# A selective scan between two feed-forward layers: one scan instruction over two rows, group sums on GpSimd, and a planner's constants with them

## The chip, the cores and the metric

The kernel runs on one core of one Trainium2 chip, in float32. The metric is the device time of one execution in microseconds (us). The kernel before has a median of 2821.96 us over 3 runs.

## What is computed

Each of the 4 x 1024 tokens has 512 values. The reference adds half of a feed-forward layer to them, then a selective state-space layer, then half of the same feed-forward layer again:

```python
x = x + 0.5 * ffn(layernorm(x))
x = x + attn(layernorm(x))
x = x + 0.5 * ffn(layernorm(x))
# ffn: silu(x @ gate_w.T * gate_s) * (x @ up_w.T * up_s) @ down_w.T * down_s,  512 -> 1408 -> 512
# attn: h, gate = split(W_in x);  h = silu(causal conv of 4 taps over time);  (ts, B, C) = rms(Wx h)
#       delta = softplus(Wdt ts + bias);  for each channel i (1024) and state n (16), over time t:
#       s[i,n] = exp(delta[i,t] * A[i,n]) * s[i,n] + delta[i,t] * B[n,t] * h[i,t]
#       y[i,t] = sum_n s[i,n] * C[n,t] + D[i] * h[i,t];   out = Wout (y * silu(gate))
```

## The kernel before

The tokens are cut into 16 chunks of 256 (T), four to a sequence. A chunk of the state-space layer is prepared (`prep`: layer norm, transposes, input projection `hp`, convolution, `sp` for ts, B and C; `heads`: delta and delta*h, called dd, written to DRAM rows and read back as `rep`, so that each of four groups of 32 partitions holds 32 channels for four of the 16 states), then scanned (`scan`), then projected back (`tail`).

In `scan` a chunk has 8 channel tiles i. A tile has 4 groups g and, in a group, 4 rows h of 256 time steps. For two rows at a time:
- ACT makes the decays (L841), one exponential for each row, into a PSUM bank `da`; there are three such banks.
- POOL (GpSimd) makes delta*h*B, 128x512, into `sb` (L848).
- DVE scans each row in place (L857, `tensor_tensor_scan`), starting from 0 in the first chunk of a sequence and from the kept state else; keeps the last column of both rows as state (L867), unless it is the last chunk of a sequence; and multiplies by C (L874).
- POOL adds the product of an odd group to that of the even group before it (L882).

What is left of a tile are two sums of 4 rows. PE folds them (L891): for either sum and each row one matmul with a 128x32 matrix adds up the four partition groups, so 8 matmuls of 256 columns into the bank `yps`, that is kept for this alone. A float32 matmul leaves two records in the profile. DVE adds D*h (L903), POOL multiplies by the gate (L909).

The feed-forward layers run in 17 passes (ORDER) over two chunks of either layer: gate products (L414), evicted by ACT (L429), Silu over `hd` in three parts (SILUS), up products (L414), evicted by DVE (L452), and the down product by Strassen's scheme (L539, L555), whose sums and differences of `hd` POOL makes (L506). DVE adds the results to x (L578). Their layer norms (`normed`) take for each tile of 128 tokens statistics on DVE (L332, L333), three tiny operations on POOL (L337 to L339), scale and shift on ACT (L350), a transpose on PE (L343) and an eviction on ACT (L358). PE's projections, the passes and the folds share four PSUM banks (class `mm`).

The order on each engine is set by a planner at build time. Every operation has an engine, a cost, what it reads and writes, and a due time; a scan unit is due by PACE, a pass by FFN_END. The planner takes the operation that can start first and, among those, the one due first; HOT is due before all others. Buffers are of classes with so many slots each (SLOTS). The result is one fixed order for each engine, in which an operation that must wait holds up what stands behind it. All transfers but the small constants are issued by SP, in the planner's order.

Of the kernel before, what the change touches and what calls it, by code (L numbers as in the profile page):

```python
# [9 lines left out]
F32 = mybir.dt.float32  # L10
AF = mybir.ActivationFunctionType
ALU = mybir.AluOpType
# [25 lines left out]
for _p in range(7, 14, 2):  # L38
    ORDER += [[(1, _p), (1, _p + 1)], [(2, _p - 6), (2, _p - 5)]]
ORDER += [[(2, _p), (2, _p + 1)] for _p in range(9, 14, 2)] + [[(2, 15)]]  # L40
SILUS = (4, 8, 11)
SLOTS = dict(
    mm=4, da=3, rf=12, rm=6, px=14, xf=4, xi=2, xo=1, xn=3, ss=2, sm=8, sr=4, u=2, dd=2, rep=2, bc=2, sn=2, sq=1, row=8, bcd=2, tsT=1, bcT=1, xnT=1,
)
PACE = 153
# [4 lines left out]
FFN_END = 2650  # L50
FLIPS = 16
HOT = -1e9

# [126 lines left out]
def macaron_kernel(ctx: ExitStack, tc: tile.TileContext, a: dict, out: bass.AP):  # L180
# [7 lines left out]
    yps = banks.tile([P, 2, T], F32, name="yps")  # L188
    ident = const.tile([P, P], F32, name="ident")
    make_identity(nc, ident)  # L190
    neg_half = const.tile([P, 4], F32, name="neg_half")
    nc.gpsimd.memset(neg_half, -0.5)
    fold = const.tile([P, Q], F32, name="fold")
# [86 lines left out]
    def scale_down(down, due):  # L280
        ds2 = Buf("px", "ds2", [P, 2, T])

        def flat():
            return ds2.tile.rearrange("p a t -> p (a t)")
# [35 lines left out]
    def normed(x, at_x, name, due, flipped):  # L320
        sm = Buf("sm", f"sm{name}", [P, 16])
        xn = Buf("xn", f"xn{name}", [P, H])
        tp = mm(f"tp{name}")
        m, q = (sm, 0), (sm, 1)

        def parts():
            s = sm.tile
            return s[:, 0:6], s[:, 6:8], s[:, 8:9], s[:, 9:10], s[:, 10:11]

        def spread():  # L330
            stt, mv, *_ = parts()
            pin(nc.vector.bn_stats(stt, at_x()))  # L332
            pin(nc.vector.bn_aggr(mv, stt))  # L333

        def roots():
            _, mv, ve, rs, nb = parts()
            pin(nc.gpsimd.tensor_scalar(ve, mv[:, 1:2], EPS, None, ALU.add))  # L337
            pin(nc.gpsimd.tensor_tensor(rs, ve, neg_half[:, 0:1], ALU.pow))
            pin(nc.gpsimd.tensor_scalar(nb, mv[:, 0:1], rs, -1.0, ALU.mult, ALU.mult))  # L339

        def turned():
            for k in range(KH):
                pin(nc.tensor.transpose(tp.tile[:, k * P : (k + 1) * P], xn.tile[:, k * P : (k + 1) * P], ident))  # L343

        dst, w, more = flipped
        op("DVE", 0.65, spread, x, [m], due - 9, name=f"stats{name}")
        op("POOL", 1.0, roots, [m], [q], due - 8, name=f"roots{name}")
        op(
            "ACT", 0.71,
            lambda: pin(nc.scalar.activation(  # L350
                xn.tile, at_x(), AF.Identity, bias=sm.tile[:, 10:11], scale=sm.tile[:, 9:10],
            )),
            list(x) + [q], [xn] + w, due - 4, name=f"xn{name}",
        )
        op("PE", 0.45, turned, [xn], [tp], due - 2, name=f"flip{name}")

        def out_of():
            pin(nc.scalar.copy(dst(), tp.tile.rearrange("p (k t) -> p k t", k=KH)))  # L358
            if more:
                more()  # L360

        op("ACT", 0.48, out_of, [tp], w, HOT, name=f"unflip{name}")

# [18 lines left out]
    def ffn(n):  # L382
# [13 lines left out]
        for v, (stage, p) in enumerate(of):  # L396
            x = x_of[p] if stage == 2 and p in x_of else Buf("xf", f"x{name}_{v}", [P, 2, H])
            pairs.append(x)
            for m in range(J):
                t, r = J * v + m, J * p + m  # L400
                due = ffn_due(base[0]) - FLIPS - 3 * (W4 - t)
                if x.cls == "xf":
# [4 lines left out]
                normed(  # L407
                    quads(x, m), lambda x=x, m=m: x.tile[:, m, :], f"{name}_{t}", due,
                    (lambda t=t: fxT[:, :, t * P : (t + 1) * P], [("fxT", t)], None),
                )  # L410
# [11 lines left out]
        for it in range(NF):  # L422
# [9 lines left out]
                [gp], [("hd", it, t) for t in ts], HOT, name=f"ungate{name}_{it}",  # L432
# [55 lines left out]
    def split_down(name, tiles, pairs, spend):  # L488
# [21 lines left out]
        for r0, r1 in ((0, 3), (3, K1)):  # L510
            q0, q1 = r0 + K1, r1 + K1
            n = r1 - r0
            v1, v2 = (lambda r0=r0, r1=r1: s1.tile[:, r0:r1, :hw]), (lambda r0=r0, r1=r1: s2.tile[:, r0:r1, :hw])
            a11, a21 = (lambda r0=r0, r1=r1: h_at(r0, r1, 0)), (lambda r0=r0, r1=r1: h_at(r0, r1, 1))
            a12, a22 = (lambda q0=q0, q1=q1: h_at(q0, q1, 0)), (lambda q0=q0, q1=q1: h_at(q0, q1, 1))
            combine(v1, a21, a22, ALU.add, h_of(r0, r1, 1) + h_of(q0, q1, 1), s_of(s1, r0, r1), n, t0 - 4 + r0, "s1")
            combine(v2, v1, a11, ALU.subtract, h_of(r0, r1, 0) + s_of(s1, r0, r1), s_of(s2, r0, r1), n, t0 + 3 + r0, "s2")
            combine(a21, a11, a21, ALU.subtract, h_of(r0, r1, 0) + h_of(r0, r1, 1), h_of(r0, r1, 1), n, t0 + 8 + r0, "s3")
# [85 lines left out]
        for r0, r1 in ((0, 3), (3, K1)):  # L604
# [3 lines left out]
                ALU.subtract, h_of(q0, q1, 0) + s_of(s2, r0, r1), h_of(q0, q1, 0), r1 - r0, t0 + 15 + r0, "s4",  # L608
# [31 lines left out]
    def prep(k):  # L640
        d = st[k]
        base = at(k - 1, 7) if k else 70.0
        xT = d["xnT"] = Buf("xnT", f"xnT{k}", [P, KH, K - 1 + T])
        for j in range(J):
# [4 lines left out]

            def edges(j=j):  # L650
# [7 lines left out]
            o = K - 1 + j * P  # L658
            normed([x], lambda x=x: x.tile, f"m{k}_{j}", base + 2 * j, (lambda o=o: xT.tile[:, :, o : o + P], [(xT, j)], None))
            op("POOL", 0.3, edges, [(xT, 1)] if j else [], [("back",)] if j else [(xT, 0), ("back",)], HOT, name=f"edges{k}_{j}")  # L660
        u = d["u"] = Buf("u", f"u{k}", [P, NI, T])
        for i in range(NI):
# [9 lines left out]
            op("ACT", 0.45, first, [hp], [(u, i)], HOT, name=f"tap{k}_{i}")  # L672
# [16 lines left out]
        sr = [Buf("sr", f"sr{k}_{j}", [P, 8]) for j in range(J)]  # L689
# [12 lines left out]
        for j in range(J):  # L702
            def squares(j=j):
                v = sp.tile.rearrange("p (j t) -> p j t", j=J)
                for q, (o, m) in enumerate(parts):
                    pin(nc.scalar.activation(sq.tile[:, o : o + m], v[:, j, o : o + m], AF.Square, accum_out=sr[j].tile[:, q : q + 1]))

            def powers(j=j):
                ss, rr = sr[j].tile[:, 0:3], sr[j].tile[:, 4:7]
                pin(nc.gpsimd.tensor_scalar(ss[:, 0:1], ss[:, 0:1], 1.0 / R, EPS, ALU.mult, ALU.add))  # L710
                pin(nc.gpsimd.tensor_scalar(ss[:, 1:3], ss[:, 1:3], 1.0 / N, EPS, ALU.mult, ALU.add))
                pin(nc.gpsimd.tensor_tensor(rr, ss, neg_half[:, 0:3], ALU.pow))

            def weigh(j=j):
                v = sp.tile.rearrange("p (j t) -> p j t", j=J)
                for q, (o, m) in enumerate(parts):
                    pin(nc.vector.scalar_tensor_tensor(
                        sn[j].tile[:, o : o + m], v[:, j, o : o + m], sr[j].tile[:, 4 + q : 5 + q], ln_w[:, o : o + m], ALU.mult, ALU.mult,
                    ))

            op("ACT", 0.6, squares, [sp], [sq, (sr[j], 0)], HOT, name=f"sq{k}_{j}")
            op("POOL", 1.4, powers, [(sr[j], 0)], [(sr[j], 1)], HOT, name=f"rr{k}_{j}")
            op("DVE", 0.54, weigh, [sp, (sr[j], 1)], [sn[j]], HOT, name=f"sn{k}_{j}")
# [82 lines left out]
    def gates(k):  # L806
        for i in range(NI):
# [5 lines left out]
                [gp], [("g", i)], HOT, name=f"ung{k}_{i}",  # L813
# [7 lines left out]
    def scan(k):  # L821
# [4 lines left out]
        for i in range(NI):  # L826
# [3 lines left out]
            made_of = []  # L830
            for g in range(NS):
                due = at(k, i * NS + g)
                for h in range(0, S, 2):
# [3 lines left out]
                    sb = Buf("px", f"sb{nm}", [P, 2, T])  # L837
                    for j in range(2):
# [7 lines left out]
                    behind("dbu", op(  # L846
                        "POOL", 1.23,
                        lambda sb=sb, h=h, g=g, rep=rep: pin(nc.gpsimd.tensor_tensor(  # L848
                            sb.tile, rep.tile[:, h : h + 2, 1, :], bc.tile[:, g : g + 1, :].to_broadcast([P, 2, T]), ALU.mult,
                        )),  # L850
                        reps + bcs, [(sb, 0), (sb, 1)], due - 6, after=last_of("dbu"), name=f"dbu{nm}",
                    ))
# [202 lines left out]
```

## Time and profile before

| what | value |
|---|---|
| median of 3 runs | 2821.96 us (2820.63 to 2824.64) |
| the profiled execution | 2822.59 us |
| its span, first to last instruction | 2820.8 us |
| PE busy | 2768.3 us |
| DVE busy | 2543.7 us |
| POOL busy | 2395.0 us |
| ACT busy | 1756.3 us |
| mean granted TensorE clock | 0.994 |

The span is what the profile covers, and all shares are of it. PE is TensorE's matmuls, PEld its weight loads, DVE VectorE, ACT ScalarE, POOL GpSimd, SP the engine that issues transfers. A row such as "L857 DVE TENSOR_TENSOR_SCAN da<-da,state,sb ... x1536 | 1090.8, 741" is a group of instructions of line 857: what it writes and reads, its count, the time in which at least one of them was busy, and the mean record of one in ns. Records of one engine overlap by some 0.08 us on DVE, so a group's busy time over its count is less than the mean; what one instruction occupies is best read from start to start in the timeline. A wait line gives the waiting engine and line, whom it waited for, the total in us, how often, and the longest.

### The profile page before, as it was taken

Reading aid. Unit: us, or ns where it says so; the run is one execution under the profiler, and the core shown is the slowest. Engines: PE = TensorE matmul, PEld = TensorE weight load, DVE = VectorE, ACT = ScalarE, POOL = GpSimd, SP = SyncE. Lnnn points to the kernel's source line nnn. Section 1 sums busy time; section 2 is a strip of 40 time slices with the busy share of each in tenths; the row PEclk is TensorE's granted clock in tenths of the full one; section 3 lists DMA queues with packets and bytes.
Section 4 is the critical chain, followed back from the end, with each engine's and each line's share of the span. In section 5 each row is a group of like instructions: output and inputs, shape, how many; then the busy total and the mean of one; then the engine's idle time right before and its main releaser. Section 6 shows DMA issues by size and latency. Waiting matters only on the chain.

```text
span 2820.8 us, 38816 instructions
## 1 busy us (share of the span) xinstructions
PE 2768.3 (98%) x11278; PEld 1733.2 (61%) x11278; DVE 2543.7 (90%) x5088; ACT 1756.3 (62%) x3286; POOL 2395.0 (85%) x2279
## 2 busy tenths in 40 slices
PE   8998999999999999999999999999999999999999
PEld 6565575575655755647557565575665756657458
DVE  3289899999999999999999999999999999999861
ACT  2356667667567585676666766668567576674821
POOL 1189899899898989899899999899899998989951
PEclk9999999999999999999999999999999999999999
DMA  8576667676576666866757667666676775766635
GB/s 263 168 206 178 168 184 219 185 214 197 148 236 158 202 185 172 233 160 189 206 162 236 168 185 207 196 175 194 173 224 173 219 208 153 211 165 176 175 102 155
DMA packets 304691, 531.01 MB, mean 188 GB/s; under 512 B 34016, under 2 KB 58720, under 8 KB 304480
## 3 DMA queue, kind: packets, MB, share of 16 engines
q1 hardware_dynamic: 303040, 528.35, 66.5%
q8 instruction: 90, 1.47, 0.2%
q14 instruction: 121, 0.99, 0.1%
q10 hardware_dynamic: 1440, 0.19, 0.0%
HBM read 464.84 MB, written 63.57 MB: 187 GB/s over the span
## 4 chain that ended last, share of the span: by engine, by line
PE 43%; DVE 35%; issue 7%; ACT 7%; POOL 5%; DMA 3%; SPq 0%; ACTq 0%; DVEq 0%; POOLq 0%
DVE da L857 21%; PE upf L414 11%; PE gatef L414 11%; DVE sb L874 6%; PE hp L633 3%; PE gp L633 3%; PE op L930 2%; PE paf L539 2%; POOL sb L848 2%; ACT da L841 2%; DVE u L676 2%; PE yps L891 2%; PE pcf L539 2%; DMA rep<-row 2%; PE pbf L539 1%
## 5 line engine op out<-in xcount | busy, mean ns | idle before, releaser
L841 ACT ACTIVATE da<-rep,a_w 128x256 f32<-128x256 f32 x2048 | 964.7, 476 | 794.8 <-DVE sb L874 734.4
L848 POOL TENSOR_TENSOR sb<-rep,bc 128x512 f32<-128x512 f32 x1024 | 1284.1, 1280 | 81.5 <-DMA rep<-row 59.2
L857 DVE TENSOR_TENSOR_SCAN da<-da,state,sb 128x256 f32<-128x256 f32 x1536 | 1090.8, 741 | 49.6 <-ACT da L841 29.5
L882 POOL TENSOR_TENSOR sb<-sb,sb 128x512 f32<-128x512 f32 x512 | 651.5, 1278 | 84.9 <-DVE sb L874 83.1
L874 DVE TENSOR_TENSOR sb<-da,bc 128x512 f32<-128x512 f32 x1024 | 692.8, 677 | 0.5
L414 PE MATMUL gatef<-fxT,w_gate_w 128*128 128x512 f32 (+1 forms) x1496 | 632.7, 574 | 5.1 <-ACT dd L772 3.0
L414 PE MATMUL upf<-fxT,w_up_w 128*128 128x512 f32 (+1 forms) x1496 | 624.3, 569 | 0.5 <-DVE u L676 0.5
L414 PEld LDWEIGHTS gatef<-fxT,w_gate_w 128*128 128x128 f32 x1496 | 284.5, 192 | 294.7 <-issue 267.6
L414 PEld LDWEIGHTS upf<-fxT,w_up_w 128*128 128x128 f32 x1496 | 280.9, 190 | 290.9 <-issue 268.0
L857 DVE TENSOR_TENSOR_SCAN da<-da,sb 128x256 f32<-128x256 f32 x512 | 333.5, 681 | 22.6 <-ACT da L841 19.5
L633 PE MATMUL hp<-xnT,w_W_in 128*128 128x259 f32 x1024 | 238.6, 383 | 4.3 <-ACT fxT L358 1.5
L633 PE MATMUL gp<-xnT,w_W_in 128*128 128x256 f32 x1024 | 241.1, 380 | 0.2 <-ACT fxT L358 0.2
L633 PEld LDWEIGHTS hp<-xnT,w_W_in 128*128 128x128 f32 x1024 | 192.4, 190 | 61.3 <-issue 20.1
L633 PEld LDWEIGHTS gp<-xnT,w_W_in 128*128 128x128 f32 x1024 | 191.9, 189 | 61.0 <-issue 28.4
L930 PE MATMUL op<-w_Wout,u 128*128 128x512 f32 x512 | 229.3, 594 | 0.0
L452 DVE SCALAR_TENSOR_TENSOR hd<-upf,up_s,hd 128x512 f32<-128x512 f32 (+1 forms) x187 | 131.0, 701 | 59.4 <-PE upf L414 59.4
L676 DVE SCALAR_TENSOR_TENSOR u<-hp,conv_w,u 128x256 f32<-128x256 f32 x384 | 171.9, 468 | 6.0 <-ACT u L668 5.3
L429 ACT ACTIVATE hd<-gatef,gate_s 128x512 f32<-128x512 f32 (+1 forms) x187 | 121.8, 652 | 64.0 <-PE gatef L414 63.8
L930 PEld LDWEIGHTS op<-w_Wout,u 128*128 128x128 f32 x512 | 95.8, 190 | 105.2 <-issue 99.4
L891 PE MATMUL yps<-sb,fold 128*32 128x256 f32 x2048 | 141.1, 387 | 0.6 <-POOL sb L882 0.5
L539 PE MATMUL paf<-w_half,hd 128*128 128x256 f32 x620 | 141.0, 380 | 0.0
L539 PEld LDWEIGHTS paf<-w_half,hd 128*128 128x128 f32 x620 | 117.1, 190 | 22.0 <-issue 4.4
(104 smaller groups left out, 2911.1 us busy)
## 6 DMA issues: line engine op xcount, KB each, us to landing
rep<-row SPq DMA_DIRECT2D x512, 256.0 KB, 5.0
w_half<-sd SPq DMA_DIRECT2D x272, 256.0 KB, 3.0
w_W_in<-in_W_in_dram SPq DMA_DIRECT2D x256, 256.0 KB, 3.9
w_gate_w<-in_gate_w_dram SPq DMA_DIRECT2D x187, 256.0 KB, 4.5
w_up_w<-in_up_w_dram SPq DMA_DIRECT2D x187, 256.0 KB, 3.6
row<-dd SPq DMA_DIRECT2D x128, 256.0 KB, 3.2
w_Wout<-in_Wout_dram SPq DMA_DIRECT2D x128, 256.0 KB, 3.8
bc<-bcd SPq DMA_DIRECT2D x64, 256.0 KB, 5.2
```

The lines of the kernel that those rows point to most:

```text
L414: pin(nc.tensor.matmul(o.tile[:, :wide], lhsT=cols(w.tile)[:, k, :], rhs=fxT[:, k, :wide], start=(k == 0), stop=(k == KH - 1),))
L452: lambda up=up, it=it: pin(nc.vector.scalar_tensor_tensor(hd[:, it, :wide], up.tile[:, :wide], up_s[:, it : it + 1], hd[:, it, :wide], ALU ...
L539: pin(nc.tensor.matmul(bank.tile[:, m * hh : (m + 1) * hh], lhsT=of(r, m), rhs=w.tile[:, h * hh : (h + 1) * hh], start=(first and m == 0 a ...
L633: pin(nc.tensor.matmul(o.tile[:, :width], lhsT=cols(w.tile)[:, kk, :], rhs=xT.tile[:, kk, lo:], start=(kk == 0), stop=(kk == KH - 1),))
L676: lambda hp=hp, i=i, q=q: pin(nc.vector.scalar_tensor_tensor(u.tile[:, i, :], hp.tile[:, q : q + T], conv_w[:, i, q : q + 1], u.tile[:, i, ...
L841: lambda da=da, j=j, h=h, g=g, rep=rep, b0=b0: pin(nc.scalar.activation(da.tile[:, j, :], rep.tile[:, h + j, 0, :], AF.Exp, scale=a_w[:, b ...
L848: lambda sb=sb, h=h, g=g, rep=rep: pin(nc.gpsimd.tensor_tensor(sb.tile, rep.tile[:, h : h + 2, 1, :], bc.tile[:, g : g + 1, :].to_broadcas ...
L857: lambda da=da, sb=sb, j=j, h=h, g=g, b0=b0: pin(nc.vector.tensor_tensor_scan(da.tile[:, j, :], da.tile[:, j, :], sb.tile[:, j, :], 0.0 if ...
L874: lambda sb=sb, da=da, g=g: pin(nc.vector.tensor_tensor(sb.tile, da.tile, bc.tile[:, NS + g : NS + g + 1, :].to_broadcast([P, 2, T]), ALU. ...
L882: "POOL", 1.23, lambda pa=pa, sb=sb: pin(nc.gpsimd.tensor_tensor(pa.tile, pa.tile, sb.tile, ALU.add)),
L891: pin(nc.tensor.matmul(yps[j * Q : (j + 1) * Q, i % 2, :], lhsT=fold, rhs=made_of[2 * g + j // 2].tile[:, j % 2, :], start=(g == 0), stop= ...
L930: pin(nc.tensor.matmul(o.tile, lhsT=u.tile[:, i, j * P : (j + 1) * P], rhs=wo[i].tile, start=(i == 0), stop=(i == NI - 1),))
```

## The change

One scan instruction of 512 columns takes the place of two of 256. So that the second row does not go on from the end of the first, ACT writes zeros into the first column of each row of decays after the exponentials (L887). The kept state then enters in another way: once for each channel tile, the decay of the first time step is made for all 16 rows (L840 and L846), the state is multiplied by it (L850), and for each group it is added to the first column of `sb` (L868).

`sb` now holds a whole group, 128x1024: POOL makes it in one instruction (L860) and adds groups in one (L917), and it also adds the two sums of a tile to one (L925). The fold has 4 matmuls, into one of the four `mm` banks; the bank `yps` is gone, and a fourth `da` bank takes its place. There are 8 buffers of 1024 instead of 14 of 512.

The layer norms are made for two tiles together: epsilon is added on DVE (L335), one power of two elements is taken on POOL (L328), and ACT makes the shift with two tiny activations more (L345, L346). The norms of ts, B and C likewise: ACT scales and adds epsilon (L711), POOL takes one power of six elements (L717). Silu has two parts instead of three. The output projection is planned in parts of two channel tiles instead of four. Evictions are due 20 us before their product's due time and no longer before all else; the Strassen sums are due earlier; PACE, FFN_END and SLOTS have other values.

```diff
-SILUS = (4, 8, 11)
-SLOTS = dict(
-    mm=4, da=3, rf=12, rm=6, px=14, xf=4, xi=2, xo=1, xn=3, ss=2, sm=8, sr=4, u=2, ...
-)
-PACE = 153
+SILUS = (6, 11)
+SLOTS = dict(mm=4, da=4, rf=12, rm=6, px=8, xf=4, xi=2, xo=1, xn=3, ss=2, sm=6, a0=2, sr=2, u=2, ...)
+PACE = 148
-FFN_END = 2650
+FFN_END = 2620
+SUMS = 20
+EV = 20
...
-            pin(nc.gpsimd.tensor_scalar(ve, mv[:, 1:2], EPS, None, ALU.add))
-            pin(nc.gpsimd.tensor_tensor(rs, ve, neg_half[:, 0:1], ALU.pow))
-            pin(nc.gpsimd.tensor_scalar(nb, mv[:, 0:1], rs, -1.0, ALU.mult, ALU.mult))
+            pin(nc.gpsimd.tensor_tensor(v[:, :, 9], v[:, :, 8], neg_half[:, 0:2], ALU.pow))
+                pin(nc.vector.tensor_scalar(s[:, 8:9], s[:, 7:8], EPS, None, ALU.add))
+                pin(nc.scalar.activation(s[:, 10:11], s[:, 6:7], AF.Identity, scale=s[:, 9:10]))
+                pin(nc.scalar.activation(s[:, 11:12], s[:, 10:11], AF.Identity, scale=-1.0))
...
-            combine(v1, a21, a22, ALU.add, ..., n, t0 - 4 + r0, "s1")
-            combine(v2, v1, a11, ALU.subtract, ..., n, t0 + 3 + r0, "s2")
-            combine(a21, a11, a21, ALU.subtract, ..., n, t0 + 8 + r0, "s3")
+            combine(v1, a21, a22, ALU.add, ..., n, t0 - SUMS + r0, "s1")
+            combine(v2, v1, a11, ALU.subtract, ..., n, t0 + 7 - SUMS + r0, "s2")
+            combine(a21, a11, a21, ALU.subtract, ..., n, t0 + 12 - SUMS + r0, "s3")
...
+            if not first:
+                a0 = Buf("a0", f"a0{k}_{i}", [P, S, NS])
+                op("DVE", 0.08, ... nc.vector.tensor_tensor(a0.tile, a_w[:, b0 : b0 + S, :], rep.tile[:, :, 0, 0:1]..., ALU.mult)
+                op("ACT", 0.1, ... nc.scalar.activation(a0.tile, a0.tile, AF.Exp)
+                op("DVE", 0.08, ... nc.vector.tensor_tensor(state[:, b0 : b0 + S, :], state[:, b0 : b0 + S, :], a0.tile, ALU.mult)
             for g in range(NS):
+                sb = Buf("px", f"sb{k}_{i}_{g}", [P, S, T])
+                    "POOL", 2.31,
+                        sb.tile, rep.tile[:, :, 1, :], bc.tile[:, g : g + 1, :].to_broadcast([P, S, T]), ALU.mult,
+                if not first:
+                            sb.tile[:, :, 0], sb.tile[:, :, 0], state[:, b0 : b0 + S, g], ALU.add,
                 for h in range(0, S, 2):
-                        "POOL", 1.23,
-                            sb.tile, rep.tile[:, h : h + 2, 1, :], bc.tile[:, g : g + 1, :].to_broadcast([P, 2, T]), ALU.mult,
+                        "ACT", 0.1, lambda da=da: pin(nc.scalar.copy(da.tile[:, :, 0], zeros)), ...
-                    for j in range(2):
-                            lambda ...: pin(nc.vector.tensor_tensor_scan(
-                                da.tile[:, j, :], da.tile[:, j, :], sb.tile[:, j, :],
-                                0.0 if first else state[:, b0 + h + j, g : g + 1], ALU.mult, ALU.add,
+                        lambda ...: pin(nc.vector.tensor_tensor_scan(
+                            da.tile.rearrange("p a t -> p (a t)"), da.tile.rearrange("p a t -> p (a t)"),
+                            sb.tile[:, h : h + 2, :].rearrange("p a t -> p (a t)"), 0.0, ALU.mult, ALU.add,
...
+            pa, pb = made_of
+            op(
+                "POOL", 2.31, lambda pa=pa, pb=pb: pin(nc.gpsimd.tensor_tensor(pa.tile, pa.tile, pb.tile, ALU.add)),
+            yp = mm(f"yp{k}_{i}")
-                for g in range(NS // 2):
                     for j in range(S):
                         pin(nc.tensor.matmul(
-                            yps[j * Q : (j + 1) * Q, i % 2, :], lhsT=fold, rhs=made_of[2 * g + j // 2].tile[:, j % 2, :],
-                            start=(g == 0), stop=(g == NS // 2 - 1),
+                            yp.tile[j * Q : (j + 1) * Q, :T], lhsT=fold, rhs=pa.tile[:, j, :], start=True, stop=True,
```

## The prediction

> **What bounds the kernel now.** I read the page first, its busy times and slices.
>
> ```profile
> span 2820.8 us, 38816 instructions
> PE 2768.3 (98%) x11278; PEld 1733.2 (61%) x11278; DVE 2543.7 (90%) x5088; ACT 1756.3 (62%) x3286; POOL 2395.0 (85%) x2279
> PEclk9999999999999999999999999999999999999999
> ```
>
> PE is busy almost throughout; its idle time is 2820.8 - 2768.3 = 52.5 us. But the shares are means over the span, and DVE and POOL have little to do at either end. The timeline has POOL's first large operation at 136.25 us, and the last fold of a scan starts at 2725.4 us. From there to the end PE has 95 us of work without a gap worth naming. So the second view is the table by stage for 131 to 2726 us, the scan's window.
>
> ```profile
> core 0: us, PE busy (x) PEld busy (x) DVE busy (x) ACT busy (x) POOL busy (x), PEclk, DMA share, GB/s
> 131.00:2726.00 2595.00, 2556.62 (x10449) 1579.12 (x10451) 2482.78 (x4952) 1705.07 (x3202) 2367.42 (x2212) 0.99 0.68 188
> ```
>
> Three engines are nearly full there: PE 98.5%, DVE 95.7% (idle 112 us), POOL 91.2% (idle 228 us). The reader is to see that what PE saves is only had if DVE and POOL fit into the shorter window too. The third view, the waits, tells who is ahead of whom.
>
> ```profile
> ACT da L841 <- DVE sb L874: 734.4, 668, 3.5
> POOL sb L882 <- DVE sb L874: 83.1, 70, 4.6
> POOL sb L848 <- DMA rep<-row: 59.2, 25, 14.7
> DVE da L857 <- ACT da L841: 49.0, 44, 4.2
> POOL sb L848 <- PE yps L891: 14.1, 7, 3.1
> PE pcf L539 <- POOL hd L506: 9.9, 2, 9.1
> ```
>
> ACT and POOL run ahead of DVE (ACT waits 734 us for a bank that DVE frees, POOL 83 us for DVE's products), and PE almost never waits for any of them. **PE sets the end, DVE is close behind, POOL has the reserve.** The change spends that reserve.
>
> **PE.** The fold of each of the 128 channel tiles is 8 matmuls, in 16 records; it becomes 4, in 8 records.
>
> ```profile
> 2648.43 1.07 PE L891 MATMUL yps<-sb,fold 128*32 128x256 f32 x16
> 2649.43 17.43 PE L414 MATMUL gatef<-fxT,w_gate_w 128*128 128x512 f32 x40
> ```
>
> From the start of a fold to the start of the next group is 1.00 us, so 62.5 ns a record. Halving gives 128 x 0.50 = **-64 us**. Bounds: 0, if a short group costs the same 1.00 us; and -79, if it shrinks to one record's 0.387 us (128 x 0.61). I take the rate, since the records are issued at an even pace. All other matmuls are the same in number and shape; moving them (the output projection now in parts of two tiles, both halves in turn) costs nothing while PE has other work, as it has now.
>
> **DVE.** Two scans of 256 become one of 512, which no row shows. In the timeline a pair with a state occupies 1.30 us and a pair from zero 1.17 us, start to next start:
>
> ```profile
> 1006.95 1.39 DVE L857 TENSOR_TENSOR_SCAN da<-da,state,sb 128x256 f32<-128x256 f32 x2
> 1008.25 0.46 DVE L676 SCALAR_TENSOR_TENSOR u<-hp,conv_w,u 128x256 f32<-128x256 f32 x1
> ...
> 200.99 1.26 DVE L857 TENSOR_TENSOR_SCAN da<-da,sb 128x256 f32<-128x256 f32 x2
> 202.16 0.15 DVE L867 COPY state<-da 128x2 f32<-128x2 f32 x1
> ```
>
> Before: 768 x 1.30 + 256 x 1.17 = 1298 us. For the new width: an add (L578) takes 420 ns at 256 and 673 at 512, so 253 per 256 columns over a fixed 167. The zero-start scan's record is 681 at 256 (L857), so 514 per 256 columns; at 512 that is 167 + 1028 = 1195 ns, less the 0.08 us by which records overlap: 1.11 us. After: 1024 x 1.11 = 1137, so -161 us. Bounds: 1.30 (nothing saved, +33) and 0.84 (the second half at the add's rate, -438).
>
> Added are 384 additions into first columns (L868), 192 small products for them (L840, L850) and 96 epsilon additions (L335): 672 tiny operations. The nearest rows are the 128x2 state copy (record 149 ns, occupying 0.05 to 0.07) and the aggregate of the statistics (182, occupying 0.10). I take 0.10, so +67; bounds 34 and 128. **DVE: -94 us**, 2389 in the window.
>
> **POOL.** The 1024 products and 512 sums of 512 columns become 512 and 256 of 1024, plus 128 sums of 1024 that are new. Rows of one line give the slope: L506 takes 1281 ns at 512 and 1821 at 768, 540 more. At 1024 that is 2361, less the 26 ns between L848's 1280 mean and its 1284.1/1024 busy: 2.335 us. After: 896 x 2.335 = 2092; before: 1284.1 + 651.5 = 1936; +156. Bounds: 2.53 (twice the old one, +331) and 2.17 (no fixed part left, +8).
>
> The small operations fall: 102.2 us for the norms' roots (L337 to L339) and 39.7 us for the three powers (L710 to L712). What stays is one power for two tiles, 48 times, and one of six elements, 16 times. One element is 571 ns and three are 861, so 145 an element: 716 and 1296 ns, 34 + 21 = 55 us; -87. **POOL: +69 us**, 2436 in the window.
>
> [...] The row: an add of 512 takes 1278 ns on POOL (L882) and 673 on DVE (L578). [...] By the rows, 128 sums of 1024 columns would cost DVE 128 x (167 + 4 x 253) ns = 151 us, 2540 in the window; with its 112 us of idle kept that is 2652, 57 longer than now, so 2880. With the sums on POOL the working below holds. [...]
>
> **ACT.** 1024 copies of two zeros into the banks, 384 further tiny activations: nearest row the 128x16 square, 187 ns (busy 173 each), 1408 x 0.175 = +246 us, bounds 141 and 296 (by the 210 ns accumulator read). The changed kernel holds 175 table loads instead of 200: -25 x 1.283 = -32. So 1756 + 214 = 1970 us, 70%: at no cost, hidden in the 734 us that ACT waits for banks. The fourth bank pays for the copy's place between the exponentials and the scan; without that cover it would be 1024 x 0.17 = 174 us on DVE's path.
>
> **Moved.** The Strassen sums fall due 9 to 16 us earlier on POOL, evictions lose their absolute precedence on ACT, the norms' roots serve two tiles and go ahead of the products. PE's waits that these touch are 9.9 us (above) and some 5 of the 14.3 us for normalised tiles; I take 0, between -15 and +15. The fold now takes one of four shared banks; a PE that must wait for the eviction costs up to 0.5 us a fold, +64, nearest to the 7.5 us that DVE waits for folds today: inside the same 15. Transfers are as many as before, in the same queue; rep's loads go with the blocks.
>
> **The sum.** The profiled execution took 2822.6 us, 1.8 outside the span, and stands 0.6 above the median 2821.96. PE alone: 2822.6 - 64 = 2758.6. POOL has to follow into a window of 2595 - 64 = 2531 us with 2436 of work: idle 95 instead of 228. Of the 228, these stay: 27 before the first products (12.7 and 14.7, for the first softplus and the first load), 45 of further waits for rep, 6 at the last sums: 78. The other 150 are POOL ahead of DVE and PE, and go to the extent that POOL becomes the late one. If a fifth stays, POOL is idle 108 us, 4.2% of its window, about the density that DVE reaches today (4.3%). That gives 2436 + 108 = 2544, 51 less than 2595: 2822.6 - 51, rounded to **2772 us**. DVE needs 2389 + 112 = 2501 and stays inside.
>
> **Rivals.**
> PE alone sets the end: 2758, and 2744 if its own 15 us of stalls go too. For it: the evenly full PE. Against it: POOL would need 96.2%.
> POOL keeps its gaps (the other side): its idle time is not reserve but the latency of its turn with DVE, since each sum waits for two products of 512 and each product for a tile that a sum or a fold frees. With all 228 us kept: 2436 + 228 = 2664, 69 later than now: 2892. It decides as soon as more than 2595 - 2436 = 159 us of idle stay, twice the 78 named. For it: sixteen tiles' worth of buffers in eight large ones, and a three-step chain of sums; against it: POOL's waits for DVE are waits of the faster for the slower, and DVE gets faster. Half-way, 115 to 150 us idle, it eats most of the gain: 2779 to 2813.
> The scan saves nothing (the change doesn't do what it says): 1.30 us a scan, DVE 2483 + 33 + 67 + 112 = 2695, 100 later: 2922. Only overlap lost at twice the width would do this; the rows' fixed parts speak against it.
>
> **Chances.** Forecast, 2759 to 2800: 0.55. PE alone, below 2759: 0.14. POOL eats most, 2800 to 2816: 0.10. Within 0.2%, about what a measurement can tell here: 0.06. POOL keeps its gaps: 0.12. Scan without gain: 0.03. So faster 0.79, same 0.06, slower 0.15. The range takes in the lower bound of PE and reaches through the half-way cases up to no gain: 2745 to 2828. A POOL step of 2.40 instead of 2.335 alone would add 58 us; that is why it is wide.
>
> **What the next profile would show.** Right: L860, L917 and L925 at 2.34 to 2.37 us; L892 near 1.19; fold records near 1024; POOL at 95% or more of its window, its waits for L909 well below 83 us; DVE's waits for ACT below 49; PE's idle time grown by 10 to 20 us. Wrong: POOL's waits for DVE as long as now, or PE waiting for POOL's sums at each fold; L892 at 1.30 or more; PE waiting for evictions.

## The result, and the profile after

| | before | after |
|---|---|---|
| median | 2823.19 us (4 runs, 2820.63 to 2824.64) | 3139.65 us (4 runs, 3122.95 to 3145.52) |
| profiled execution / span | 2822.59 / 2820.8 us | 3139.16 / 3137.4 us |
| mean granted TensorE clock | 0.994 | 0.961 |

The change makes the kernel slower: the ratio is 1.111 (95% interval 1.107 to 1.116). The prediction had the sign wrong.

Busy times and the clock's slices, from the page of the changed kernel:

```profile
span 3137.4 us, 36653 instructions
PE 2829.1 (90%) x10254; PEld 1738.0 (55%) x10254; DVE 2878.6 (92%) x4736; ACT 1942.2 (62%) x4652; POOL 2496.6 (80%) x1321
PEclk9999999998999998999999999999999999999999
```

DVE, which was to lose 94 us, has 335 more (2878.6 - 2543.7). PE's share falls from 98% to 90%. The table by stage, for the window of the prediction and for its middle (the last fold of a scan now starts at 3035 us, so the first row leaves out the end):

```profile
core 0: us, PE busy (x) PEld busy (x) DVE busy (x) ACT busy (x) POOL busy (x), PEclk, DMA share, GB/s
131.00:2726.00 2595.00, 2336.19 (x8495) 1426.56 (x8494) 2514.35 (x4159) 1706.80 (x4120) 2220.93 (x1162) 0.96 0.60 171
300.00:2400.00 2100.00, 1889.24 (x6855) 1149.98 (x6854) 2058.18 (x3377) 1386.31 (x3343) 1801.09 (x942) 0.96 0.60 171
```

In the middle DVE is busy for 98% of the time, PE for 90, POOL for 86. The engine that sets the pace is now DVE; the chain of work that ended last says the same:

```profile
DVE 60%; PE 24%; issue 5%; ACT 4%; POOL 3%; DMA 3%; SPq 0%; DVEq 0%; ACTq 0%; POOLq 0%
```

Which of DVE's instructions it is, the groups tell (count, busy us, mean ns of one):

```profile
L892 DVE TENSOR_TENSOR_SCAN da<-da,sb 128x512 f32<-128x512 f32 x1024 | 1216.1, 1217 | 32.1 <-ACT da L887 14.8 <-POOL sb L860 8.6 <-ACT da L881 0.5
L860 POOL TENSOR_TENSOR sb<-rep,bc 128x1024 f32<-128x1024 f32 x512 | 1203.4, 2359 | 36.1 <-DMA rep<-row 24.7 <-PE yp L933 10.5 <-DMA w_up_w<-in_up_w_dram 0.7
L917 POOL TENSOR_TENSOR sb<-sb,sb 128x1024 f32<-128x1024 f32 x256 | 603.6, 2358 | 208.4 <-DVE sb L909 153.8 <-DVE sb L868 46.7 <-DVE state L850 5.3
L868 DVE TENSOR_TENSOR sb<-sb,state 128x4 f32<-128x4 f32 x384 | 329.8, 877 | 6.5 <-POOL sb L860 5.7
L902 DVE COPY state<-da 128x2 f32<-128x2 f32 x768 | 117.3, 153 | 1.2
L840 DVE TENSOR_TENSOR a<-a_w,rep 128x16 f32<-128x16 f32 x96 | 110.1, 1147 | 5.6 <-DMA rep<-row 5.6
L850 DVE TENSOR_TENSOR state<-state,a 128x16 f32<-128x16 f32 x96 | 81.7, 851 | 0.0
```

The scan is as predicted (1217 ns a record against 1195), POOL's large operations too (2358 against 2361). But the 384 additions of 128x4 elements (L868) take 877 ns each, those of 128x16 (L840, L850) 1147 and 851, while the copy of 128x2 (L902), which reads PSUM, still takes 153. These 576 instructions are busy for 329.8 + 110.1 + 81.7 = 521.6 us; the prediction had 576 x 0.10 = 58. And the means hide a spread: L868's shortest record is 145 ns, its median 498, its longest 4418; L840's 156, 370 and 9076.

What the long ones have in common is seen when two engines' timelines of the same stretch are laid side by side. DVE first (start in us, us of the record):

```profile
1021.55 1.21 DVE L892 TENSOR_TENSOR_SCAN da<-da,sb 128x512 f32<-128x512 f32 x1
1022.68 9.08 DVE L840 TENSOR_TENSOR a<-a_w,rep 128x16 f32<-128x16 f32 x1
1031.68 1.22 DVE L892 TENSOR_TENSOR_SCAN da<-da,sb 128x512 f32<-128x512 f32 x1
...
1033.46 0.16 DVE L850 TENSOR_TENSOR state<-state,a 128x16 f32<-128x16 f32 x1
...
1038.90 1.93 DVE L868 TENSOR_TENSOR sb<-sb,state 128x4 f32<-128x4 f32 x1
```

Then POOL:

```profile
1021.76 1.84 POOL L506 TENSOR_TENSOR hd<-hd 128x768 f32<-128x768 f32 x1
1023.53 2.37 POOL L860 TENSOR_TENSOR sb<-rep,bc 128x1024 f32<-128x1024 f32 x1
1025.84 1.29 POOL L506 TENSOR_TENSOR hd<-hd 128x512 f32<-128x512 f32 x1
1027.05 2.37 POOL L917 TENSOR_TENSOR sb<-sb,sb 128x1024 f32<-128x1024 f32 x1
1029.35 2.37 POOL L860 TENSOR_TENSOR sb<-rep,bc 128x1024 f32<-128x1024 f32 x1
1034.75 0.72 POOL L950 TENSOR_TENSOR u<-u,g 128x256 f32<-128x256 f32 x1 [3.03 <-DVE u L944]
...
1038.45 2.36 POOL L860 TENSOR_TENSOR sb<-rep,bc 128x1024 f32<-128x1024 f32 x1
1040.77 2.33 POOL L917 TENSOR_TENSOR sb<-sb,sb 128x1024 f32<-128x1024 f32 x1
```

POOL works without a gap from 1021.76 to 1031.72. L840 starts at 1022.68, inside the first of these five instructions, and ends at 1031.76, when the last of them has ended. L850 starts at 1033.46, in POOL's gap of 3.03 us, and takes 0.16. L868 starts at 1038.90 inside an instruction of POOL that ends at 1040.81, and ends at 1040.83, though POOL's next instruction starts at 1040.77. So it goes throughout: of the 576, those that start while POOL is idle take 157 to 168 ns on average, the others 1.1 to 1.3 us; 323 take more than 250 ns, and each of these ends within 80 ns of the end of a POOL instruction. Mostly it is the end of one instruction. Of the 323, 291 end with the POOL instruction inside which they start, although in 230 of these cases the next one followed at once; 28 start in the last 60 ns of one and end with the next; only 4, L840 above among them, wait through rows of three to five. Nine of the 576 took 147 to 167 ns with more than 250 ns of a POOL instruction still to run: six beside one of POOL's powers of two or six elements (L328, L717), three within 11 ns of the start of a large one.

**The theory.** L868, L840 and L850 read both of their inputs from SBUF; in the scan's window all other DVE operations of two tensors, in either kernel, read at least one from PSUM. A DVE instruction with two inputs in SBUF waits here for the large POOL instruction that is running (291 of the 323 long records), and in rare cases for some of those directly behind it (4 of them). By what means it is held, no trace shows. **The rivals:** tiny instructions cost this much in any case; the joined scan, the zero copies or the changed planner constants cost the time; POOL itself is the bound.

### The profile page after: what moved, and what is told of

It reads as the page before. It is cut to its first block, busy times and chain, and to the rows that moved or that the text cites. A ratio compares the mean times of both kernels' runs of the same rounds, so it can differ in the third digit from the quotient of the medians.

```text
span 3137.4 us, 36653 instructions
## 1 busy us (share of the span) xinstructions
PE 2829.1 (90%) x10254; PEld 1738.0 (55%) x10254; DVE 2878.6 (92%) x4736; ACT 1942.2 (62%) x4652; POOL 2496.6 (80%) x1321
## 4 chain that ended last, share of the span: by engine, by line
DVE 60%; PE 24%; issue 5%; ACT 4%; POOL 3%; DMA 3%; SPq 0%; DVEq 0%; ACTq 0%; POOLq 0%
DVE da L892 25%; DVE sb L909 12%; DVE sb L868 7%; PE gatef L414 6%; PE upf L414 5%; DVE u L679 3%; DVE state L850 2%; DVE hd L452 2%; PE gp L633 2%; PE hp L633 2%; DVE a L840 2%; PE pbf L539 2%; PE op L971 2%; PE pcf L539 2%; DVE xf L578 2%
## 5 line engine op out<-in xcount | busy, mean ns | idle before, releaser
L892 DVE TENSOR_TENSOR_SCAN da<-da,sb 128x512 f32<-128x512 f32 x1024 | 1216.1, 1217 | 32.1 <-ACT da L887 14.8
L860 POOL TENSOR_TENSOR sb<-rep,bc 128x1024 f32<-128x1024 f32 x512 | 1203.4, 2359 | 36.1 <-DMA rep<-row 24.7
L917 POOL TENSOR_TENSOR sb<-sb,sb 128x1024 f32<-128x1024 f32 x256 | 603.6, 2358 | 208.4 <-DVE sb L909 153.8
L414 PE MATMUL upf<-fxT,w_up_w 128*128 128x512 f32 (+1 forms) x1496 | 646.3, 584 | 34.1 <-DVE hd L452 16.3
L868 DVE TENSOR_TENSOR sb<-sb,state 128x4 f32<-128x4 f32 x384 | 329.8, 877 | 6.5 <-POOL sb L860 5.7
L925 POOL TENSOR_TENSOR sb<-sb,sb 128x1024 f32<-128x1024 f32 x128 | 301.8, 2358 | 1.0
L633 PE MATMUL hp<-xnT,w_W_in 128*128 128x259 f32 x1024 | 254.3, 399 | 34.0 <-DVE xo L980 10.3
L633 PE MATMUL gp<-xnT,w_W_in 128*128 128x256 f32 x1024 | 253.5, 393 | 22.7 <-DVE hd L452 8.5
L887 ACT COPY da<-zeros 128x2 f32<-128x2 f32 x1024 | 166.2, 162 | 23.8
L539 PE MATMUL paf<-w_half,hd 128*128 128x256 f32 x620 | 152.4, 401 | 21.2 <-DVE xf L578 17.5
L950 POOL TENSOR_TENSOR u<-u,g 128x256 f32<-128x256 f32 x128 | 93.3, 730 | 92.5 <-DVE u L944 78.4
```

Source lines behind the costliest of these rows:

```text
L414: pin(nc.tensor.matmul(o.tile[:, :wide], lhsT=cols(w.tile)[:, k, :], rhs=fxT[:, k, :wide], start=(k == 0), stop=(k == KH - 1),))
L539: pin(nc.tensor.matmul(bank.tile[:, m * hh : (m + 1) * hh], lhsT=of(r, m), rhs=w.tile[:, h * hh : (h + 1) * hh], start=(first and m == 0 a ...
L633: pin(nc.tensor.matmul(o.tile[:, :width], lhsT=cols(w.tile)[:, kk, :], rhs=xT.tile[:, kk, lo:], start=(kk == 0), stop=(kk == KH - 1),))
L860: lambda sb=sb, g=g, rep=rep: pin(nc.gpsimd.tensor_tensor(sb.tile, rep.tile[:, :, 1, :], bc.tile[:, g : g + 1, :].to_broadcast([P, S, T]), ...
L868: "DVE", 0.07, lambda sb=sb, g=g, b0=b0: pin(nc.vector.tensor_tensor(sb.tile[:, :, 0], sb.tile[:, :, 0], state[:, b0 : b0 + S, g], ALU.add,)),
L892: lambda da=da, sb=sb, h=h: pin(nc.vector.tensor_tensor_scan(da.tile.rearrange("p a t -> p (a t)"), da.tile.rearrange("p a t -> p (a t)"), ...
```

## The experiments

Each ratio stands against the kernel before on the same chip (medians 2822 to 2823.5 us), with its 95% interval.

**e1: the state in PSUM.** The changed kernel; the state lies in a PSUM bank (so `da` has three), and ACT makes the first decays in four small exponentials, so L840 is gone.

```diff
-    state = const.tile([P, NI * S, NS], F32, name="state")
+    bank = banks.tile([P, 512], F32, name="bank")
+    state = bank[:, 0 : NI * S * NS].rearrange("p (b g) -> p b g", g=NS)
...
-                    "DVE", 0.08, lambda a0=a0, rep=rep, b0=b0: pin(nc.vector.tensor_tensor(
-                        a0.tile, a_w[:, b0 : b0 + S, :], rep.tile[:, :, 0, 0:1].to_broadcast([P, S, NS]), ALU.mult,
...
-                    "ACT", 0.1, lambda a0=a0: pin(nc.scalar.activation(a0.tile, a0.tile, AF.Exp)), [a0], [a0], at(k, i * NS) - 8,
...
+                    for h in range(S):
+                        pin(nc.scalar.activation(a0.tile[:, h, :], a_w[:, b0 + h, :], AF.Exp, scale=rep.tile[:, h, 0, 0:1]))
```

> The changed kernel with the state kept in PSUM: each of the 480 small DVE operations L868 and L850 then has one input in SBUF and one in PSUM; the 96 products L840 are left out, their exponentials are made by four small ACT operations of 128x4 each; the PSUM bank for the state is taken from the decays (three banks instead of four). Theory (a DVE operation with two SBUF inputs waits until GpSimd's running operation ends): the two groups fall from 877 and 851 ns to about 155, DVE's busy time from 2879 to about 2395 us, and the time to 2760 to 2830, since PE and POOL then set the end. Rival 1 (such narrow operations cost 0.85 us whatever they read): they stay at 850 ns, the time at 3030 or more. Rival 2 (the rest of the change, its order and its banks, makes the loss): the operations get short, but the time stays over 2950.

Measured 2884.58 us, 1.0215 (1.0198 to 1.0232): 255 us less than the changed kernel. The group of the same 384 additions:

```profile
L865 DVE TENSOR_TENSOR sb<-sb,bank 128x4 f32<-128x4 f32 x384 | 50.2, 155 | 28.4 <-POOL sb L857 26.8
```

155 ns in place of 877, with POOL as busy as before; the longest takes 165. The same shape, the same count, the same engine: for this group only where one input lies has changed. (e1 as a whole also has one `da` bank fewer and no L840, so its 255 us are not the wait of this group alone.) That the tiny operations are dear in themselves is refuted. But the kernel is still 61 us slower than before, which the theory did not foresee.

**e2: the state by pointer.** The changed kernel, four `da` banks; instead of L840, L850 and L868, one `tensor_scalar` for each row makes sb + state * decay on one element of a partition, with decay and sb as scalar pointers.

```diff
-                            sb.tile[:, :, 0], sb.tile[:, :, 0], state[:, b0 : b0 + S, g], ALU.add,
...
+                        for h in range(S):
+                            pin(nc.vector.tensor_scalar(
+                                sb.tile[:, h, 0:1], state[:, b0 + h, g : g + 1], a0.tile[:, h, g : g + 1], sb.tile[:, h, 0:1], ALU.mult, ALU.add,
```

> The changed kernel with four decay banks and the state in SBUF as it is, but each row's first column is made by a tensor_scalar of one element a partition (state times decay plus column, the last two as pointers to scalars): 1536 small DVE operations in place of 480; the 96 products L840 go to ACT as in the run before. Theory: an operation with one tensor input and pointers takes no part in the wait, so about 150 ns each, occupying 0.065: +100 us in place of 522, DVE busy about 2460 us, time 2780 to 2850. Rival 1 (narrow operations cost 0.85 us each): 1536 x 0.85, time above 3800. Rival 2 (the rest of the change): over 2950 with short operations.

Measured 2919.90 us, 1.0341 (1.0325 to 1.0356).

```profile
L860 DVE TENSOR_SCALAR sb<-state,a,sb 128x1 f32<-128x1 f32 x1536 | 301.6, 262 | 12.3 <-POOL sb L850 12.3
```

These operations, with everything in SBUF but only one input as a tensor, did not wait for POOL: all 1536 took 236 to 281 ns, 262 on average. The time is above the 2780 to 2850 expected, because its own price was set too low: 1536 x 0.20 us of DVE where 0.065 was foreseen, and DVE again is full (2051.92 of the middle 2100 us).

**e3 and e4: the wait by itself.** The kernel before, with 384 useless multiplications of 128x4 added to DVE, whose result nobody reads. In e3 both inputs lie in SBUF (the first of the two lines of operands), in e4 one lies in PSUM (the second).

```diff
+                    if h == 0 and not first:
...
+                                spare, state[:, b0 : b0 + S, g], a_w[:, b0 : b0 + S, g], ALU.mult,
+                                spare, da.tile[:, 0, 0:S], a_w[:, b0 : b0 + S, g], ALU.mult,
```

> The kernel before plus 384 multiplications of 128x4 on DVE, one a group behind its first scans, both inputs in SBUF, the result used by nothing. Theory: each waits for GpSimd's running operation, here 1.25 us instead of 2.34 and running 91% of the time, so about half the excess of the changed kernel, 0.4 us: mean 500 to 600 ns, DVE +160 to 200 us, time 2900 to 3000. Rival 1 (narrow operations are slow by themselves): 850 ns each, +310 us, and the same in the next run. Rival 2 (only the rest of the change matters): 150 ns, time within 30 us of before.

> As the run before, but one of the two inputs is the PSUM bank of the decays; count, size, place in the order and result are the same. Theory: about 150 ns each, occupying 0.07: DVE +27 us, time 2825 to 2855. Rival 1: 850 ns each, time as in the run before, above 2950. Rival 2: as the theory.

e3: 2996.76 us, 1.061 (1.0595 to 1.0626). e4: 2841.27 us, 1.0061 (1.0046 to 1.0076). The group in e3:

```profile
L867 DVE TENSOR_TENSOR spare<-state,a_w 128x4 f32<-128x4 f32 x384 | 240.3, 626 | 0.0
```

And in e4:

```profile
L867 DVE TENSOR_TENSOR spare<-da,a_w 128x4 f32<-128x4 f32 x384 | 58.2, 152 | 0.8
```

Nothing of the change is in these two. The input in SBUF instead of PSUM costs 155 us of the kernel's time. (That e4 takes 18 us longer than the kernel before, for 28 us more of DVE's busy time, shows how little room DVE has.) The 229 long ones of e3 all end with a POOL instruction, 5 of them after waiting through more than one; those that start beside a running one take 734 ns on average, the others 150. POOL's instructions here are half as long as in the changed kernel (1.28 against 2.36 us), and the mean with POOL running is smaller in the same sense (734 against 1111 for L868). The theory stands.

The two also tell what to make of the clock, 0.961 in the changed kernel. e3 has the matmuls of the kernel before, yet its granted clock is 0.983 and PE is busy for 2826.0 us; in e4 the clock is 0.996 and PE busy for 2771.2. So a lower clock and a longer PE come with DVE's waits here, and the changed kernel's 2829.1 us of PE, with 1024 records fewer than before, are no sign of a cause of their own.

**e5: no zero copies.** e1, with ACT's 1024 zero copies gone: ACT sets the first delta of each row to 200 once for each tile (`zeros` holds 200 here), so that the exponential itself gives 0.

```diff
+                "ACT", 0.17, lambda rep=rep: pin(nc.scalar.copy(rep.tile[:, :, 0, 0], zeros)), ...
...
-                        "ACT", 0.1, lambda da=da: pin(nc.scalar.copy(da.tile[:, :, 0], zeros)), [], [(da, 0), (da, 1)], due - 5,
```

> The run with the state in PSUM (2884.6 us), without its 1024 copies of zeros: once for each channel tile ACT writes 200 over the first column of delta, after the first decays are made from it, so that the exponentials there are exp(-100) or less. What is left of the loss is, in theory 1, ACT between DVE and three banks: DVE waits 116 us for the zeros' line there. Then 166 us of ACT's work go, DVE's wait for ACT falls below 60 us and the time to 2820 to 2850. Theory 2 (planner's constants and the order they make): within 10 us of 2885. Theory 3 (GpSimd's long operations and their chain): within 15 us of 2885, with the waits for GpSimd unchanged.

Measured 2824.75 us, 1.0005 (0.9995 to 1.0014): 60 us less than e1. In e1 DVE waited 116.0 us for a zero copy (L884), 69 times; here its waits for ACT's decays are 69.4. The wait lines of e1 and then of e5:

```profile
DVE da L889 <- ACT da L884: 116.0, 69, 4.5
```

```profile
DVE da L889 <- ACT da L882: 69.4, 54, 5.3
```

So with three banks the copies are on the path, which explains what e1 kept. Whether they cost something with four banks was not tried by itself.

**e6: the scan part undone.** The changed kernel with two scans of 256 from the state, without first columns and zero copies; all else (1024-wide POOL work, folds of 4, norms, constants, four banks) as changed.

```diff
-                            da.tile.rearrange("p a t -> p (a t)"), da.tile.rearrange("p a t -> p (a t)"),
-                            sb.tile[:, h : h + 2, :].rearrange("p a t -> p (a t)"), 0.0, ALU.mult, ALU.add,
...
+                    for j in range(2):
...
+                                da.tile[:, j, :], da.tile[:, j, :], sb.tile[:, h + j, :],
+                                0.0 if first else state[:, b0 + h + j, g : g + 1], ALU.mult, ALU.add,
```

> The changed kernel with the scan part alone undone: two scans of 256 with the kept state as a pointer, no copies of zeros, no first columns; four banks, GpSimd's 1024-wide operations, all sums on GpSimd, the short fold and the constants as in the changed kernel. DVE gets 2543.7 + 6 us. If the loss lies in the scan part alone: 2770 to 2815, below the kernel before, by PE's 64 us less what GpSimd's fuller window takes. If the rest loses by itself (GpSimd's chain, the fold in the shared banks, the constants): 2840 or more.

Measured 2821.21 us, 0.9992 (0.9982 to 1.0001): no change, between the two expectations. The loss is all in the scan part. But PE's relief brings nothing either, with 96 us more work on POOL (2491.3): PE is busy 2732.2 us, 36 less than before, and idle 88 instead of 52. DVE, at 2561.3 us, is as full as it was.

**e7: the old constants.** e1 with PACE, FFN_END, SILUS, the sums' due times and the evictions' precedence of the kernel before.

> The run with the state in PSUM (2884.6 us), with the planner's constants of the kernel before: PACE 153, FFN_END 2650, Silu in three parts, the Strassen sums' due times and evictions before all else. If the constants of the change cost: 2820 to 2860. If they help or do nothing: 2875 to 2910.

Measured 2904.43 us, 1.0287 (1.0271 to 1.0302): 20 us more than e1. The new constants are no cause of the loss.

**e8: odd rows on ACT.** A joined scan that leaves DVE alone: the even row starts from the state as the scan's initial value, and for the odd row ACT makes sb + state * decay in one operation with two pointers; its first decay is 0 through delta, as in e5. Four banks, no DVE operation with two inputs in SBUF.

```diff
+                        for h in range(1, S, 2):
+                            pin(nc.scalar.activation(
+                                sb.tile[:, h, 0:1], state[:, b0 + h, g : g + 1], AF.Identity, bias=sb.tile[:, h, 0:1], scale=a0.tile[:, h, g : g + 1],
...
+                            0.0 if first else state[:, b0 + h, g : g + 1], ALU.mult, ALU.add,
```

> The changed kernel with the scan over two rows kept, but no DVE operation with two SBUF inputs, four banks and the state in SBUF: the even row of a pair starts from its state by the scan's own pointer, the odd row's first column is made by one ACT operation (state times decay plus column), and the odd rows' zero comes from an exponential of a delta set to 200, so that the copies of zeros go. DVE: the two-scans run's 2561 us less 768 x 0.12 and 256 x 0.05, about 2460; PE and GpSimd as there (2732, 2491); ACT about 2000. Theory (all three full engines must be relieved together; each part alone brings nothing): 2770 to 2805, below the kernel before. Rival (GpSimd's fuller queue takes PE's 64 us whatever DVE does): 2815 to 2835. Rival (ACT between GpSimd and DVE becomes the late one): over 2835.

Measured 2815.64 us, 0.9978 (0.9969 to 0.9987); missed: 6 us of gain where the least foreseen was 17. DVE is at 2440.2 us, 103 below the kernel before, PE at 2720.3, 48 below; yet PE is idle 92 us.

**e9: POOL relieved.** e8, but every second tile is folded by 8 matmuls again, without POOL's sum: 144 us less on POOL (2346.1), 23 more on PE (2743.1).

```diff
+            one = i % 2 == 0
+            if one:
                 "POOL", 2.31, lambda pa=pa, pb=pb: pin(nc.gpsimd.tensor_tensor(pa.tile, pa.tile, pb.tile, ALU.add)),
...
+            whole = [pa] if one else [pa, pb]
...
+                            yp.tile[j * Q : (j + 1) * Q, :T], lhsT=fold, rhs=b.tile[:, j, :], start=(n == 0), stop=(n == len(whole) - 1),
```

> The run before with GpSimd relieved: for every second channel tile the two sums are not added on GpSimd but folded both on PE, in 8 matmuls as in the kernel before: GpSimd -64 x 2.35 = -150 us, PE +32. If GpSimd's queue is what holds the run before: 15 to 40 us shorter than it. If PE sets the end there: 25 to 35 us longer.

Measured 2829.67 us, 1.0026 (1.0016 to 1.0035): 14 us more than e8, between the two expectations. If POOL alone set the end, 144 us less of it would show as a gain.

**e10: the scan part alone.** The kernel before with the scan of e8 and nothing else of the change: DVE 2439.8 us, 104 less, PE untouched.

> The kernel before with that scan part alone (one scan of two rows, even row by pointer, odd row by ACT), three banks, GpSimd's operations of 512 columns, fold and constants of before: DVE about 2444 us in place of 2544, PE and GpSimd unchanged. Theory (PE sets the end of the kernel before): within 10 us of 2822. Rival (DVE sets it): 2740 to 2780.

Measured 2825.61 us, 1.0010 (1.0001 to 1.0019), PE 2772.5 us or 98%. DVE's relief alone, with 250 us more work on ACT (2006.7), is worth nothing. That fits PE as what sets the end of the kernel before, as the prediction said.

**e11 and e12: evictions first.** e8 and e9 with the evictions before all else again, as in the kernel before.

```diff
-EV = 20
+EV = 1e9
```

> The run with the odd rows on ACT (2815.6 us), with the evictions before all else on ACT, as in the kernel before; nothing else differs. There PE is busy 48 us less than before and idle 40 us more, in many waits of at most a few us, partly for ACT. If the evictions' lost precedence makes PE's new waits: 10 to 35 us shorter. If GpSimd's queue, 97% busy between 300 and 2400 us, sets the end: within 8 us of 2816, with PE's waits moved to its sums.

> The run with half of the tiles folded by PE alone (2829.7 us; GpSimd busy 83% of its span), with the evictions before all else. There nothing but PE is near full, yet PE is idle 81 us. If the evictions' place makes that: 2795 to 2815. If not: within 8 us of 2830.

e11: 2808.26 us, 0.9958 (0.9946 to 0.9971), the fastest kernel of the study, faster than the kernel before and the changed one. e12: 2821.34 us, 0.9996 (0.9987 to 1.0005). The order is worth 7 to 8 us in both, less than the 10 and 15 foreseen at least. e11 falls to its other expectation, that POOL's queue sets the end; but PE's waits have not moved to POOL's sums as that one had it (8.3 us in e11), and e12, with POOL relieved, is slower. The busy times on e11's page, and its window in the table by stage, here to 2706 us, since the last fold starts at 2704.7 instead of 2725.4:

```profile
PE 2715.4 (97%) x10254; PEld 1696.5 (60%) x10254; DVE 2442.4 (87%) x4160; ACT 2032.7 (72%) x4618; POOL 2490.1 (89%) x1321
```

```profile
131.00:2706.00 2575.00, 2498.42 (x9400) 1537.62 (x9399) 2379.83 (x4010) 1976.40 (x4511) 2472.24 (x1292) 0.99 0.66 190
```

POOL has 2472 us of work in 2575 and is idle for 103, PE is idle for 77. e12's busy times:

```profile
PE 2745.2 (97%) x10766; PEld 1717.2 (61%) x10766; DVE 2437.2 (86%) x4160; ACT 2030.0 (72%) x4612; POOL 2345.9 (83%) x1257
```

## Why the prediction was wrong, point by point

**The step that failed** is DVE's: "672 tiny operations ... I take 0.10, so +67; bounds 34 and 128". The two rows it was taken from, the state copy and the aggregate, have one input and cannot show what a second one in SBUF does beside POOL. Of the 672, the 96 epsilon additions (one input) took 154 ns a record, as such rows say; the 576 with two inputs took 521.6 us of DVE. At 158 ns a record they would have been busy for 91, so some 430 us are waiting for POOL, a term that the sum did not have; its bound for all 672 was 128. e1 and e4 show the cause by moving one input.

**The sum with DVE's measured time.** DVE's busy time was to be 2543.7 - 94 = 2450; it is 2878.6, so 429 more, about what the waits come to. The prediction had 2501 us of need for DVE in a window of 2544, a reserve of 43: 2772 + 429 - 43 = 3158, where 3139 was measured. The other engines then wait for DVE: POOL waits 153.8 us for its products at L917 (83.1 before), ACT 114.1 us for L840, and PE idles. The rival "the scan saves nothing" had DVE as the bound, but by another mechanism, and too small.

**The scan**: right. From start to start 1.12 us against 1.11. In e1, where nothing waits for POOL, DVE is busy 2460.1 us, 84 less than before, against the -94 predicted; its own 576 tiny operations (L865, L847 and the 96 epsilon additions) are busy for 81 (67 was foreseen for 672).

**PE's fold**: right in kind, a little less: a fold takes 0.57 us from its start to the next group instead of 1.00, 0.43 saved where 0.50 was foreseen, -55 us instead of -64. Of that PE's busy time shows 53 in e11, 48 in e8 and 36 in e6, at granted clocks of 0.995, 0.992 and 0.988; why the clock differs was not tried.

**ACT**: 1942 us against 1970, with enough cover in total. That the fourth bank pays for the zero copies was not tried alone; with three banks they cost 60 us (e1 to e5).

**POOL**: mis-sized by 26 us. Predicted +69, measured 2490.1 - 2395.0 = +95 (e11), of which the large operations are 1208.6 + 606.1 + 303.0 - 1935.6 = +182 instead of +156: 2.364 us a step, not 2.335, 896 times. The record came out right, but the 26 ns taken off for overlap are not there at this width. The small operations came out (a power of two elements takes 706 ns, predicted 716; one of six 1332, predicted 1296), but some 10 us of what they save lie outside the window (POOL's work outside it is 27.6 us before and 17.9 in e11). So POOL has 2472 us in it, not 2436.

**Would it have been 2772 without the wait? In no kernel tried.** The kernels with the change's work on POOL that have neither the wait, nor e2's extra work on DVE, nor the zero copies take 2808 to 2825 us (e5, e6, e8, e11). In e11 the prediction's form comes close: 2472 of work and the idle time of 108 that it chose make 2580, where 2575 was measured. That is 20 less than 2595, of which the stretch behind the last fold gives 6 back (101.7 us instead of 95.4). By that form, POOL's 36 us more of work are most of what is missing from the 51. But that POOL is what holds e11 is not shown, and the form's closeness may be luck: with 144 us less on POOL (e12) the kernel takes 13 us longer, and PE's idle time falls only from 91 us to 77 (2822.6 - 2745.2), while PE's work grows by 30. What can be said is where the gain went: PE is busy 53 us less in e11 than before, and 38.5 of them come back as idle time (52.5 to 91.0), in many short waits, the longest 9.6 us for a normalised tile of ACT. From 300 to 2400 us PE and POOL of e11 are 97% full and DVE 94%, and it seems that what one of them is late with reaches the next through the fixed order of each engine. This was argued, not tried; which of the hand-overs would have to be loosened stays open.

**The signs named beforehand**: L892 near 1.19 and L860, L917 at 2.34 to 2.37 came true and say nothing on the outcome. The sign for a wrong forecast, POOL's waits for DVE as long as now, came true (153.8). PE's waits at the fold (20.1 us for POOL's sums) are a consequence of the same.

## What to carry to other kernels

Before adding even tiny VectorE operations of two tensors beside a busy GpSimd, look where both inputs lie. With one in PSUM, with the others as scalar pointers, or on ACT, they cost here their own 0.15 to 0.38 us each; with both in SBUF they took 0.63 us (e3) to 1.15 us (L840) on average, since most of those that began beside a large GpSimd instruction lasted to its end, and a few to the end of one further behind. A price taken from a row has to come from operands in the same memories, not only of the same shape. In this kernel, with three engines above 90% full, PE's relief (e6, with more work for POOL) and DVE's (e10) were each worth nothing by itself, and both together, with the old order of the evictions, brought 14 us where PE had 53 less to do (e11).

## What was not expected of the hardware

- One DVE instruction of 128x16 elements lasted 9.08 us, from inside one POOL instruction to the end of the fifth in a row; in e3 the longest was 9.59 us. Such rows are rare, 4 of 323 and 5 of 229 long records; of the other 319 in the changed kernel 291 ended with the POOL instruction beside which they began, and 28, begun in its last 60 ns, with the next. POOL's own records do not lengthen: L860 takes 2357 ns on average beside one of these DVE instructions and 2361 without.
- POOL's powers of two or six elements did not hold DVE up: ten of the 576 additions and products of the changed kernel began beside one and took 149 to 174 ns, among them a 128x4 addition that began with 1255 ns of a power of six (L717) still to run and took 167.
- A `tensor_scalar` of one element a partition takes 262 ns with two pointers (e2) and 154 with constants (L335).
- An ACT operation of one element with scale and bias by pointer takes 375 ns (e8), one with scale alone 284 (L345; as much with four elements in e1).
